# Conditional layer on quarters of TensorE, and contexts issued with every second group's scores

## The chip, the cores and the metric

The kernel runs on one core of a Trainium2 chip. Time is the device time of one execution in microseconds (us). The core has a matrix engine (TensorE, PE in the profile, with its weight loads as PEld), a vector engine (VectorE, DVE), an activation engine (ScalarE, ACT), GpSimd (POOL) and a queue engine (SyncE, SP) that issues most DMAs. Each works through its own instructions in order and waits on semaphores for the others. PE writes its results to banks of the memory PSUM, from which DVE and ACT copy them to the on-chip memory SBUF.

## The reference, cut to what matters

```python
def cond(x, condition, weights):               # x: (64, 64, 1024)
    W = weights[condition]                     # one (64, 64) matrix for each of 64 batches
    return einsum('bct,bcd->bdt', x, W)
def attn(x, qkvw, qkvb, ow, ob):               # 32 heads of 32, attention over the 64 rows of a batch
    q, k, v = split(x @ qkvw + qkvb)
    probs = softmax(einsum('bhqd,bhkd->bhqk', q, k) / sqrt(32))
    return einsum('bhqk,bhkd->bhqd', probs, v) @ ow + ob
x = x + attn(cond(x, itok_B_0_15, weights))
x = x + ffn(cond2(x, itok_B_0_7))              # routed LoRA layer, then a quantized gated FFN
```

Everything is float32 apart from the quantized products. The change lies in `cond` and in the attention; what follows the attention is left as it is.

## The kernel before, in words

The 4096 rows (64 batches of 64) are worked in eight blocks of 512 rows, that is four tiles of 128 rows; a tile holds two batches. The function `attention` does all that is spoken of here.

The conditional layer of a block (`conditional`, lines 337 to 376) multiplies each tile with the matrices of its two batches. These stand as two 64x64 blocks on the diagonal of a 128x128 tile `wbd`, zero elsewhere, so that one 128x128 matmul serves both batches (line 350). A product is half a tile's columns: four such matmuls into one PSUM bank, eight products for a block. The results are copied to the quarters B11, B12, B21 and B22 of the block's activations, those of even tiles by DVE (line 356), of odd ones by ACT (line 358). Four sums T1 to T4 of these quarters follow on DVE (lines 366 and 371).

The projections to queries, keys and values use a Strassen-Winograd scheme: seven products of quarter matrices instead of eight, in the order 1, 6, 7, 5, 2, 4, 3 (`job`, line 378). Product 1 needs B11 and the weights' A11, product 6 needs T2 and the weights' sum S2, product 7 T3 and S3, product 5 T1 and S1, product 2 B21 and A12. They share four PSUM banks a, b, c, d. A query or key job (`rows_job`, line 428) has seven products of 4 matmuls, a value job (`values_job`, line 455) seven of 8. In block 0 the sums S1 to S4 of the raw weights are made on the way, four on one another (`sums`, lines 270 to 273), on DVE or POOL, and stored for the later blocks.

The attention itself goes by groups, two for each of four steps c of a block: `scores` (16 matmuls of 64x64, four of them side by side on the four quarters of the array, line 491), then on DVE and ACT a softmax (lines 503 to 515), a transposition by DMA (line 526, with copies on ACT at lines 521 and 533), then `context` (16 matmuls of 128x64, two side by side, line 543). ACT copies a context out and sends it to DRAM (lines 553 and 554). The pool of its copies `co` has two buffers, that of the turned probabilities `pT` four, that of the contexts' PSUM banks two.

What stands where in each engine's instruction order is set by a planner written out in the file. `run` keeps a planned time `now` and adds each product's planned cost; before each product it issues whatever is due by that time (`at`). A product's copies out of PSUM, its `rest`, are issued only after the next product (`behind`). A group begins at its due time: first its scores, then every context whose probabilities are ready.

The four-bank pool `ps_g` is a ring that the conditional layer and all projections share: a product that wants a bank waits until what lay in it has been copied out. In the last step of a block the fills are the next block's conditional layer, its first value job and its first query and key jobs; in the last block of all they are the first products of the output projection, with the last contexts at a fixed planned time (`at(now + 41, contexts)`, line 699).

```python
                    ps = ps_g.tile([P, 4, P], F32, tag="g", name=f"cond_{b}_{j}_{hf}")
                    for q in range(KQ):
                        k = hf * KQ + q
                        nc.tensor.matmul(ps[:, q, :], xt[:, k * P:(k + 1) * P], wbd[j], start=True, stop=True)
```

## Time and profile before

| what | value |
|---|---|
| time of three runs | 2479.37, 2483.23, 2483.56 us (median 2483.23) |
| time of the profiled execution | 2482.55 us, its span 2480.8 us |
| PE busy | 2435.7 us (98%), 13232 matmul records |
| DVE busy | 1524.9 us (61%) |
| ACT busy | 953.6 us (38%) |
| conditional layer on PE (line 350) | 512 records of 128x128, 62.5 us |
| scores (line 491), contexts (line 543) | 2048 records each, 70.7 and 73.5 us |

A float32 matmul appears as two records. "Busy" counts a matmul to its modelled end. An idle time in the views is given with the instruction that ended it.

### The profile page before, as it was taken

Reading aid. Unit: us, or ns where it says so; the run is one execution under the profiler, and the core shown is the slowest. Engines: PE = TensorE matmul, PEld = TensorE weight load, DVE = VectorE, ACT = ScalarE, POOL = GpSimd, SP = SyncE. Lnnn points to the kernel's source line nnn. Section 1 sums busy time; section 2 is a strip of 40 time slices with the busy share of each in tenths; the row PEclk is TensorE's granted clock in tenths of the full one; section 3 lists DMA queues with packets and bytes.
Section 4 is the critical chain, followed back from the end, with each engine's and each line's share of the span. In section 5 each row is a group of like instructions: output and inputs, shape, how many; then the busy total and the mean of one; then the engine's idle time right before and its main releaser. Section 6 shows DMA issues by size and latency. Waiting matters only on the chain.

```text
span 2480.8 us, 34182 instructions
## 1 busy us (share of the span) xinstructions
PE 2435.7 (98%) x13232; PEld 1703.8 (69%) x13232; DVE 1524.9 (61%) x2957; ACT 953.6 (38%) x1303; POOL 360.8 (15%) x451
## 2 busy tenths in 40 slices
PE   8999999999999999999999999999999999999996
PEld 7888888888888888888888644444454545454452
DVE  4585585675764755745646623333367777778787
ACT  1243353443443533533534533343423333333333
POOL 5010011011122221110000233334200000000001
PEclk9999999999999999999999999999999999999997
DMA  8795767676677667766646668877744443434343
GB/s 281 262 266 153 225 192 232 191 208 203 205 201 246 206 188 248 201 202 181 171 145 215 187 213 248 271 232 239 227 151 79 87 79 81 85 73 91 71 96 70
DMA packets 417980, 446.76 MB, mean 180 GB/s; under 512 B 299665, under 2 KB 353938, under 8 KB 404114
## 3 DMA queue, kind: packets, MB, share of 16 engines
q1 hardware_dynamic: 387298, 377.90, 52.5%
q0 software_dynamic: 12080, 49.82, 7.6%
q10 hardware_dynamic: 18432, 16.79, 2.0%
q8 instruction: 106, 1.74, 0.3%
q14 instruction: 64, 0.52, 0.1%
HBM read 272.97 MB, written 100.66 MB: 151 GB/s over the span
## 4 chain that ended last, share of the span: by engine, by line
PE 95%; DVE 3%; DMA 1%; issue 1%; ACT 0%; SPq 0%; ACTq 0%; DVEq 0%
PE pska L428 5%; PE psva L455 5%; PE poc L1019 5%; PE pskc L428 4%; PE psvc L455 4%; PE pskd L428 4%; PE psqd L428 4%; PE pbc L1019 4%; PE pba L1019 4%; PE psvd L455 4%; PE psqa L428 4%; PE poa L1019 4%; PE pod L1019 4%; PE pbd L1019 4%; PE psqc L428 4%; PE s L491 3%
## 5 line engine op out<-in xcount | busy, mean ns | idle before, releaser
L533 ACT COPY pT<-phT 128x1024 int16<-128x1024 int16 x128 | 167.2, 1342 | 84.8 <-DMA phT<-ph 84.6
L553 ACT ACTIVATE co<-c,bqkv 128x256 f32<-128x256 f32 x128 | 60.6, 473 | 295.2 <-PE c L543 253.6
L503 DVE TENSOR_REDUCE mx<-s 128x8 f32<-128x512 f32 x128 | 88.3, 690 | 138.0 <-PE s L491 128.4
L521 ACT COPY ph<-prob 128x1024 int16<-128x1024 int16 x128 | 131.4, 1046 | 43.4 <-DVE prob L515 42.7
L414 DVE SCALAR_TENSOR_TENSOR kbd<-pskd,bqkv,psku 32x256 f32<-32x256 f32 x256 | 122.6, 479 | 30.9 <-PE pskd L428 27.2
L507 ACT ACTIVATE prob<-prob 128x512 f32<-128x512 f32 x128 | 78.9, 628 | 154.4 <-DVE prob L504 130.6
L1140 POOL TENSOR_TENSOR xo<-xo,ob 128x1024 f32<-128x1024 f32 x32 | 82.5, 2597 | 375.7 <-DMA xo<-in_x_dram 371.2
L428 PE MATMUL psqa<-yB,wq 128*128 128x256 f32 x512 | 123.5, 384 | 0.0
L428 PE MATMUL pska<-yB,wk 128*128 128x256 f32 x512 | 122.6, 382 | 0.0
L1483 POOL DMA_DIRECT2D out_dram<-y x29 | 25.2, 869 | 653.4 <-DVE y L1475 653.4
L1114 ACT COPY xh<-xo 128x1024 int16<-128x1024 int16 x64 | 64.1, 1040 | 143.8 <-DVE xo L1159 143.4
L455 PE MATMUL psva<-wv,yB 128*128 128x256 f32 x512 | 117.7, 383 | 0.0
L1019 PE MATMUL poa<-woA,cx 128*128 128x512 f32 x256 | 115.3, 593 | 0.0
L1019 PE MATMUL pba<-wtA,x1T 128*128 128x512 f32 x256 | 115.1, 592 | 0.0
L1125 ACT COPY xTo<-xhT 128x1024 int16<-128x1024 int16 x64 | 84.8, 1341 | 64.1 <-DMA xhT<-xh 62.3
L455 PEld LDWEIGHTS psva<-wv,yB 128*128 128x128 f32 x512 | 96.8, 191 | 13.4
L428 PEld LDWEIGHTS pska<-yB,wk 128*128 128x128 f32 x512 | 96.0, 190 | 14.3 <-issue 1.4
L428 PEld LDWEIGHTS psqa<-yB,wq 128*128 128x128 f32 x512 | 95.2, 190 | 13.7 <-issue 0.2
L513 DVE TENSOR_REDUCE den<-prob 128x8 f32<-128x512 f32 x128 | 86.8, 678 | 17.4 <-ACT prob L507 17.2
L504 DVE TENSOR_TENSOR prob<-s,mx 128x512 f32<-128x512 f32 x128 | 88.6, 692 | 9.7 <-DVE mx L503 0.9
L515 DVE TENSOR_TENSOR prob<-prob,den 128x512 f32<-128x512 f32 x128 | 89.8, 702 | 4.4
L412 ACT ACTIVATE kbd<-pska,bqkv 32x256 f32<-32x256 f32 x128 | 59.6, 466 | 79.2 <-PE pska L428 77.6
(243 smaller groups left out, 5138.5 us busy)
## 6 DMA issues: line engine op xcount, KB each, us to landing
wv<-v_d SPq DMA_DIRECT2D x98, 512.0 KB, 3.8
wq<-q_d SPq DMA_DIRECT2D x28, 1792.0 KB, 8.1
wk<-k_d SPq DMA_DIRECT2D x28, 1792.0 KB, 8.2
x<-in_x_dram SPq DMA_DIRECT2D x32, 512.0 KB, 9.8
ctx_d<-co ACTq DMA_DIRECT2D x128, 128.0 KB, 5.6
cx<-ctx_d SPq DMA_DIRECT2D x16, 1024.0 KB, 7.0
xo<-in_x_dram SPq DMA_DIRECT2D x32, 512.0 KB, 5.7
xT_d<-xTo SPq DMA_DIRECT2D x64, 256.0 KB, 4.1
```

The lines of the kernel that those rows point to most:

```text
L414: nc.vector.scalar_tensor_tensor(dst, ps, bias, u, ALU.add, ALU.add)
L428: nc.tensor.matmul(ps[:, 0:HB], A[:, SLOT[A_OF[i]], k, :], B[B_OF[i]][:, k, :], start=first and k == 0, stop=k == KQ - 1, skip_group_check ...
L455: nc.tensor.matmul(ps[:, j * VC:(j + 1) * VC], B[B_OF[i]][:, k, j * P:(j + 1) * P], A[:, k, :], start=first and j == 0 and k == 0, stop=k ...
L503: nc.vector.tensor_reduce(mx_v, ps, AX.X, ALU.max)
L504: nc.vector.tensor_tensor(p.rearrange("p (a e) k -> p a e k", a=2), ps, mx_v.unsqueeze(3).to_broadcast([P, 2, HPC, C]), ALU.subtract)
L513: nc.vector.tensor_reduce(den, p, AX.X, ALU.add)
L515: nc.vector.tensor_tensor(p, p, den.unsqueeze(2).to_broadcast([P, n, C]), ALU.mult)
L521: nc.scalar.copy(h, planes(p.rearrange("p n k -> p (n k)")))
L533: nc.scalar.copy(planes(pT.rearrange("p a b q -> p (a b q)")), hT)
L1019: self.nc.tensor.matmul(ps, self.B[self.B_OF[i]][:, k, :], self.A[self.A_OF[i]][:, k, :], start=first and k == 0, stop=k == self.KQ - 1, s ...
L1125: nc.scalar.copy(planes(xT.rearrange("p k q -> p (k q)")), hT)
L1140: nc.gpsimd.tensor_add(s["x"][:, t, :], s["x"][:, t, :], self.ob)
```

## The change

Each conditional product is now a whole tile: for each of eight column blocks, four 64x64 matmuls on the four quarters of the array, straight from the gathered matrices. It fills two banks, one for each batch of the tile, and is emptied by two DVE and two ACT copies of half the size. `wbd`, its clearing and its copies are gone. The sums T1 to T4 all stand after the last tile's copies. The planned cost of a tile is 1.2 where its two halves had 0.95 each; a block's first value job so has all seven products ahead of the second group of that step, where it had six.

A group issues the last product's copies right after its scores, and contexts only if two or more are ready. Their copies on ACT are spread in planned time. `pT` has six buffers, `co` a pool of its own with four. In block 0 the weight sums are issued one or two at a time between products, and the first query job takes its products in the order 1, 2, 6, 7, 5, 4, 3. The last contexts stand 3.5 later in planned time, one product of the output projection.

```diff
-        pTp = pool(ctx, "pT1", 4, side="right")
+        pTp = pool(ctx, "pT1", 6, side="right")
+        cop = pool(ctx, "co1", 4, side="right")
...
-        def sums(eng, at):
-            eng.tensor_tensor(at("S1"), at("A21"), at("A22"), ALU.add)
-            eng.tensor_tensor(at("S2"), at("S1"), at("A11"), ALU.subtract)
-            eng.tensor_tensor(at("S3"), at("A11"), at("A21"), ALU.subtract)
-            eng.tensor_tensor(at("S4"), at("A12"), at("S2"), ALU.subtract)
+        def sums(eng, at, stored):
+            def last():
+                eng.tensor_tensor(at("S4"), at("A12"), at("S2"), ALU.subtract)
+                stored()
+            return [
+                lambda: eng.tensor_tensor(at("S1"), at("A21"), at("A22"), ALU.add),
+                lambda: eng.tensor_tensor(at("S2"), at("S1"), at("A11"), ALU.subtract),
+                lambda: eng.tensor_tensor(at("S3"), at("A11"), at("A21"), ALU.subtract),
+                last,
+            ]
...
-        first_sums = [load_qk(0, "q", 0), load_qk(0, "k", 0, nc.gpsimd)]
+        first_sums = load_qk(0, "q", 0) + load_qk(0, "k", 0, nc.gpsimd)
-        first_sums.append(load_v_raw(0, nc.gpsimd))
-        wbd = []
-        for j in range(PB):
-            t = w.tile([P, P], F32, tag=f"wbd{j}", name=f"wbd{j}")
-            nc.vector.memset(t, 0.0)
-            wbd.append(t)
+        first_sums += load_v_raw(0, nc.gpsimd)
...
-            def one(hf, j):
-                key = f"B{hf + 1}{j // 2 + 1}"
-                box = []
+            def one(j):
+                banks = []
                 def product():
-                    xt = tiles[j][0]
-                    if j % 2 == 0:
-                        B[key] = yp.tile([P, KQ, HB], F32, tag=key, name=f"y{key}_{b}")
-                    ps = ps_g.tile([P, 4, P], F32, tag="g", name=f"cond_{b}_{j}_{hf}")
-                    for q in range(KQ):
-                        k = hf * KQ + q
-                        nc.tensor.matmul(ps[:, q, :], xt[:, k * P:(k + 1) * P], wbd[j], start=True, stop=True)
-                    box.append(ps)
+                    xt, wg = tiles[j]
+                    for r in range(2):
+                        banks.append(ps_g.tile([P, KC, C], F32, tag="g", name=f"cond{r}_{b}_{j}"))
+                    for k in range(KC):
+                        for r, f in ((0, 0), (1, 1), (0, 1), (1, 0)):
+                            nc.tensor.matmul(
+                                banks[r][halves[f], k, :], xt[halves[r], k * P + f * C:k * P + (f + 1) * C],
+                                wg[halves[r], :], start=True, stop=True,
+                            )
                 def rest():
-                    dst = B[key][:, :, (j % 2) * P:(j % 2 + 1) * P]
-                    if j % 2 == 0:
-                        nc.vector.tensor_copy(dst, box[0])
-                    else:
-                        nc.scalar.copy(dst, box[0])
-                    if (hf, j) == (0, 3):
+                    for hf in range(2):
+                        key = f"B{hf + 1}{j // 2 + 1}"
+                        if j % 2 == 0:
+                            B[key] = yp.tile([P, KQ, HB], F32, tag=key, name=f"y{key}_{b}")
+                        for r in range(2):
+                            t0 = (j % 2) * P + r * C
+                            src = banks[r][:, hf * KQ:(hf + 1) * KQ, :]
+                            if r == 0:
+                                nc.vector.tensor_copy(B[key][:, :, t0:t0 + C], src)
+                            else:
+                                nc.scalar.copy(B[key][:, :, t0:t0 + C], src)
+                    if j == PB - 1:
                         t_of("T1", "B12", "B11")
-                    elif (hf, j) == (1, 3):
                         t_of("T2", "B22", "T1")
                         t_of("T3", "B22", "B12")
-                    elif (hf, j) == (1, 1):
                         B["T4"] = B["B12"]
                         nc.vector.tensor_tensor(B["T4"], B["B21"], B["T2"], ALU.subtract)
-                return 0.95, product, rest
+                return 1.2, product, rest
             def t_of(key, x, y):
                 B[key] = yp.tile([P, KQ, HB], F32, tag=key, name=f"{key}_{b}")
                 nc.vector.tensor_tensor(B[key], B[x], B[y], ALU.subtract)
-            for j, (_, wg) in enumerate(tiles):
-                for r in range(2):
-                    (nc.gpsimd if b else nc.vector).tensor_copy(wbd[j][halves[r], halves[r]], wg[halves[r], :])
-            return [one(0, j) for j in range(PB)] + [one(1, j) for j in (2, 3, 0, 1)]
...
+        def job(name, cost, n, matmuls, put, begin=None, done=None, order=ORDER):
...
-                    if i == ORDER[0] and begin:
+                    if i == order[0] and begin:
                         begin()
+                    if order[1] == i == 2:
+                        behind.pop()()
...
-            return [one(i) for i in ORDER]
+            return [one(i) for i in order]
...
-        def context(b, c, us, pTs):
+        def context(b, c, us, pTs, wait):
...
-            for n, u in enumerate(us):
+            def copied(n, u):
                 m, t = UNITS[u]
                 ch = m * NP + c
-                co = p2.tile([P, HB], F32, tag="co", name=f"co_{b}_{c}_{u}")
+                co = cop.tile([P, HB], F32, tag="co", name=f"co_{b}_{c}_{u}")
                 nc.scalar.activation(co, pc[:, n, :], AF.Identity, bias=bqkv[:, 2 * KC + ch:2 * KC + ch + 1])
                 nc.scalar.dma_start(ctx_d[2 * b + t][:, ch, :], co)
+            for n, u in enumerate(us):
+                if wait:
+                    at(now + wait, lambda n=n, u=u: copied(n, u))
+                else:
+                    copied(n, u)
...
-        def contexts():
-            while waiting and len(waiting[0][3]) == 2:
-                context(*waiting.pop(0))
+        def contexts(least=1):
+            ready = sum(len(pTs) == 2 for *_, pTs in waiting)
+            for n in range(ready if ready >= least else 0):
+                context(*waiting.pop(0), 1.7 * n * (least - 1))
         def group(b, c, us):
             def begin():
                 ps = scores(b, c, us)
-                contexts()
+                if behind:
+                    behind.pop()()
+                contexts(2)
                 pTs = []
                 waiting.append((b, c, us, pTs))
...
-                        f = load_qk(*qk_jobs[n + 2])
-                        if f:
-                            pending_sums.append(f)
-                js = rows_job(b, c, wh, next_load)
+                        pending_sums.extend(load_qk(*qk_jobs[n + 2]) or [])
+                js = rows_job(b, c, wh, next_load, (1, 2, 6, 7, 5, 4, 3) if n == 0 else ORDER)
                 if b == 0 and n >= 2:
-                    cost, product, rest = js[5]
-                    def product_and_sums(product=product):
-                        product()
-                        if pending_sums:
-                            pending_sums.pop(0)()
-                    js[5] = (cost, product_and_sums, rest)
+                    for at_, count in ((5, 2), (6, 2)):
+                        with_sums(js, at_, pending_sums, count)
                 fills += js
             return fills
...
                 nxt = (b, g + 1) if g + 1 < NV else (b + 1, 0)
                 if nxt[0] < NBLK:
                     load_v(*nxt, slot)
             js = values_job(b, g, next_load)
             if (b, g) == (0, 0):
-                cost, product, rest = js[4]
-                def product_and_sums():
-                    product()
-                    pending_sums.pop(0)()
-                js[4] = (cost, product_and_sums, rest)
+                with_sums(js, 4, pending_sums, 4)
             return js
         for f in conditional(0, x_next):
...
                     if c == 0:
                         fills[7:7] = v_fill(b, 1)
                         if b == 0:
-                            cost, product, rest = fills[4]
-                            def with_sums(product=product):
-                                product()
-                                v_raw.pop()()
-                            fills[4] = (cost, with_sums, rest)
+                            for at_ in range(3, 7):
+                                with_sums(fills, at_, v_raw, 1)
                 elif b + 1 < NBLK:
                     fills += conditional(b + 1, x_next) + v_fill(b + 1, 0) + qk_fill(b + 1, 0)
...
                     op.open_rest()
                     fills += op.pair(0) + op.pair(1)
                     length = 24
-                    at(now + 41, contexts)
+                    at(now + 44.5, contexts)
                 if b + 1 == NBLK and c == 1:
                     assert next(chores, None) is None
                     early.close()
```

More of the change, by code (lines that the diff above doesn't have):

```diff
@@ L284, in load_qk @@
                     nc.sync.dma_start(t[:, SLOT[key], :, :], quarter(key, (0 if wh == "q" else H) + c * P, P))
-                def rest():
-                    sums(eng or nc.vector, lambda key: t[:, SLOT[key], :, :])
-                    nc.gpsimd.dma_start(qk_d[wh, c], t)
-                return rest
+                return sums(
+                    eng or nc.vector, lambda key: t[:, SLOT[key], :, :], lambda: nc.gpsimd.dma_start(qk_d[wh, c], t)
+                )
             nc.sync.dma_start(t, qk_d[wh, c])
@@ L303, in load_v_raw, with stored @@
                 nc.sync.dma_start(at(key), quarter(key, 2 * H + g * VC, VC))
-            def rest():
-                sums(eng, at)
+            def stored():
                 for slot in range(7):
                     later.append(lambda slot=slot: nc.gpsimd.dma_start(v_d[g][:, slot, :, :], w_v[0, g, slot]))
-            return rest
+            return sums(eng, at, stored)
         bqkv = act.tile([P, 3 * KC], F32, tag="bqkv", name="bqkv")
         x_next = load_x(0)
-        first_sums = [load_qk(0, "q", 0), load_qk(0, "k", 0, nc.gpsimd)]
+        first_sums = load_qk(0, "q", 0) + load_qk(0, "k", 0, nc.gpsimd)
         nc.sync.dma_start(bqkv, a["qkvb_t"])
-        first_sums.append(load_v_raw(0, nc.gpsimd))
-        wbd = []
-        for j in range(PB):
-            t = w.tile([P, P], F32, tag=f"wbd{j}", name=f"wbd{j}")
-            nc.vector.memset(t, 0.0)
-            wbd.append(t)
+        first_sums += load_v_raw(0, nc.gpsimd)
         kbd, vbd = [], []
@@ L337, in conditional @@
         def conditional(b, tiles):
-            def one(hf, j):
-                key = f"B{hf + 1}{j // 2 + 1}"
-                box = []
+            def one(j):
+                banks = []
                 def product():
-                    xt = tiles[j][0]
-                    if j % 2 == 0:
-                        B[key] = yp.tile([P, KQ, HB], F32, tag=key, name=f"y{key}_{b}")
-                    ps = ps_g.tile([P, 4, P], F32, tag="g", name=f"cond_{b}_{j}_{hf}")
-                    for q in range(KQ):
-                        k = hf * KQ + q
-                        nc.tensor.matmul(ps[:, q, :], xt[:, k * P:(k + 1) * P], wbd[j], start=True, stop=True)
-                    box.append(ps)
-                def rest():
-                    dst = B[key][:, :, (j % 2) * P:(j % 2 + 1) * P]
-                    if j % 2 == 0:
-                        nc.vector.tensor_copy(dst, box[0])
-                    else:
-                        nc.scalar.copy(dst, box[0])
-                    if (hf, j) == (0, 3):
+                    xt, wg = tiles[j]
[6 more added lines that the diff above has]
+                                wg[halves[r], :], start=True, stop=True,
+                            )
+                def rest():
+                    for hf in range(2):
[10 more added lines that the diff above has]
+                    if j == PB - 1:
@@ L371, in t_of @@
                 nc.vector.tensor_tensor(B[key], B[x], B[y], ALU.subtract)
-            for j, (_, wg) in enumerate(tiles):
-                for r in range(2):
-                    (nc.gpsimd if b else nc.vector).tensor_copy(wbd[j][halves[r], halves[r]], wg[halves[r], :])
-            return [one(0, j) for j in range(PB)] + [one(1, j) for j in (2, 3, 0, 1)]
-        def job(name, cost, n, matmuls, put, begin=None, done=None):
+            return [one(j) for j in range(PB)]
+        def job(name, cost, n, matmuls, put, begin=None, done=None, order=ORDER):
             banks, u = {}, {}
@@ L414, in biased, with rows_job @@
                 nc.vector.scalar_tensor_tensor(dst, ps, bias, u, ALU.add, ALU.add)
-        def rows_job(b, c, wh, next_load):
+        def rows_job(b, c, wh, next_load, order=ORDER):
             qT = None
@@ L445, in done @@
                     next_load()
-            return job(f"ps{wh}{{}}_{b}_{c}", 1.72, HB, matmuls, put, begin, done)
+            return job(f"ps{wh}{{}}_{b}_{c}", 1.72, HB, matmuls, put, begin, done, order)
         def values_job(b, g, next_load):
@@ L627, in next_load, with with_sums, product_and_sums @@
                     if n + 2 < len(qk_jobs):
-                        f = load_qk(*qk_jobs[n + 2])
-                        if f:
-                            pending_sums.append(f)
-                js = rows_job(b, c, wh, next_load)
+                        pending_sums.extend(load_qk(*qk_jobs[n + 2]) or [])
+                js = rows_job(b, c, wh, next_load, (1, 2, 6, 7, 5, 4, 3) if n == 0 else ORDER)
                 if b == 0 and n >= 2:
-                    cost, product, rest = js[5]
-                    def product_and_sums(product=product):
-                        product()
-                        if pending_sums:
-                            pending_sums.pop(0)()
-                    js[5] = (cost, product_and_sums, rest)
+                    for at_, count in ((5, 2), (6, 2)):
+                        with_sums(js, at_, pending_sums, count)
                 fills += js
             return fills
+        def with_sums(fills, i, sums, count):
+            cost, product, rest = fills[i]
+            def product_and_sums():
+                for _ in range(min(count, len(sums))):
+                    sums.pop(0)()
+                product()
+            fills[i] = (cost, product_and_sums, rest)
         v_raw = []
@@ L650, in next_load @@
                     if slot == SLOT[A_OF[ORDER[-1]]]:
-                        v_raw.append(load_v_raw(g + 1, nc.vector))
+                        v_raw.extend(load_v_raw(g + 1, nc.vector))
                     return
```

## The prediction

> **What bounds the kernel now.** I first read busy times, and the chain that ended last.

> ```profile
> PE 2435.7 (98%) x13232; PEld 1703.8 (69%) x13232; DVE 1524.9 (61%) x2957; ACT 953.6 (38%) x1303; POOL 360.8 (15%) x451
> ...
> PE 95%; DVE 3%; DMA 1%; issue 1%; ACT 0%; SPq 0%; ACTq 0%; DVEq 0%
> ```

> TensorE sets the time, so only its own work and its waits count. Its waits:

> ```profile
> PE cond L350 <- DVE wbd L375: 9.2, 1, 9.2
> ...
> PE c L543 <- ACT pT L533: 5.9, 1, 5.9
> ...
> PE cond L350 <- DVE yB L356: 3.2, 7, 0.5
> PE psqd L428 <- DVE qT L414: 3.0, 1, 3.0
> ```

> (Total us, times, longest.) Apart from 1.6 us in the first query job and the kernel's very end these are nearly all, and the seven of 0.5 us lie in the very stage that the change speeds up. Here is that stage in block 4, as the chain of work shows it (start, us, what):

> ```profile
> 696.69 1.08 PE s L491 x32
> ...
> 697.79 0.70 DVE mx L503
> ...
> 698.59 0.69 DVE prob L504
> 699.28 0.38 DVE kbd L414
> ...
> 701.18 0.69 DVE yB L356
> ...
> 702.58 0.69 DVE prob L504
> 703.27 0.61 DVE yB L356
> ...
> 703.92 2.94 PE cond L350 x24
> ```

> For 6 us the chain is on DVE, not on PE. In the 17 us from 696.6 DVE is busy for most of it (columns: length, then PE, PEld, DVE, ACT, POOL busy):

> ```profile
> 696.60:713.60 17.00, 16.55 (x161) 15.30 (x161) 14.97 (x23) 9.01 (x13) 1.83 (x4) 1.00 0.53 175
> ```

> **The change part by part.** The sum is made against the profiled execution, 2482.55 us, which lies 0.7 below the median of the runs.

> *Quarter matmuls, PE alone.* PE's rows in the timeline of this stage (start, length):

> ```profile
> 696.62 1.10 PE L491 MATMUL s<-kbd,qT 64*64 64x128 f32 x32
> 697.66 1.15 PE L543 MATMUL c<-pT,vbd 128*64 128x64 f32 x32
> 698.74 4.73 PE L350 MATMUL cond<-wbd,x 128*128 128x128 f32 x40
> ...
> 706.70 3.65 PE L455 MATMUL psva<-wv,yB 128*128 128x256 f32 x16
> ...
> 710.19 3.62 PE L455 MATMUL psvb<-wv,T 128*128 128x256 f32 x16
> ```

> and, in a window only 21 ns wide (615.345 to 615.366), four score matmuls that start in it:

> ```profile
> 615.35 0.34 PE L491 MATMUL s<-kbd,qT 64*64 64x128 f32 x4
> ```

> Four quarters start together. Contexts, 64 columns like the new matmuls, take 32 records as 16 pairs in 1.15 - 0.22 (the last one's length) = 0.93 us, 58 ns a pair. A new tile is 8 column blocks x 2 records = 16 such slots: 0.93 us, 3.8 us a block with a switch of tiling at 0.1. Now a block takes 706.70 - 698.74 = 7.96. PE alone would save 4.1 us a block, 33 in all. [...]

> *What DVE and ACT make of it.* I lay the stage out from the scores' start (block 4: 696.62 = 0), in the order in which the changed program issues. PE: scores 1.03, two contexts (now one) to 3.05, tile 0 to 4.0, tile 1 to 5.0. Each tile has two banks of four, so tile 2 needs tile 0's copies done, tile 3 tile 1's. DVE: the key job's last four copies come first now, 4 x 0.48, to 2.3; max and subtract 0.69 + 0.69 with gaps, to 3.8; two copies of tile 0 to 5.1 (0.42 each, the 128x256 row of line 402, since the new copies have 256 elements; a half of line 356's 0.69 would be 0.34, taken as the low end); max, subtract to 6.6; tile 1 to 7.5; sum, reciprocal, multiply (0.68, 0.20, 0.69) to 9.2; tile 2 to 10.1, tile 3 to 11.0; T1 and T2 (1.22 each) to 13.5. ACT: context copy plus DMA issue 0.87 each, two to 3.8 (from 2.1), exponent to 4.5, tile 0 (0.36 each, line 399) to 5.3, two more context copies to 7.0, exponent 7.7, tile 1 to 8.5. So tile 2 starts at 5.3, tile 3 at 8.5 instead of 6.2; the value job wants tile 2's first bank (10.1) and starts at 10.15, its product 6 at 13.64, when product 1 (3.49) is done and T2 just so. Before, product 6 starts at 710.19 - 696.62 = 13.57 with one context in front. Without contexts (2.02 after, 1.08 before) that is 11.62 against 12.49: 0.9 us saved of 4.1. Six blocks have this form: 5.2. In block 1 no context stands there and the layout gives product 6 at 13.26 against 12.49: 0.8 lost. Sum -4.4. With DVE and ACT copies of 0.36 and 0.30 product 6 comes at 13.2, with 0.46 and 0.42 at 14.0: ends -7.5 and -2. If DVE's cover ended there, T2 would be late next, and each us of it is PE's.

> The late tail on DVE (T3, T4, then the second unit's sum and multiply at 17.7 instead of 12.1) puts its transposition behind by 5.6 us; its context starts some 20 us later, so that is hidden. The removed `wbd` copies stood on POOL, idle there: nothing. SP gets one value load earlier in its order, which waits for a product that PE has by then done: nothing.

> *Start.* PE waits to 9.19 for `wbd`; the gather itself lands at 8.67. Tiles 0 and 1 then run at the half clock (granted until 12.1), tile 3 ends near 14.3 (17.82 now). Product 1 ends at 16.1, product 2 waits for ACT's copy of bank a and ends at 18.4; DVE has the four sums (2.75) and the copies ahead of T1 and T2, so T2 is ready at 20.4 and product 6 starts at 20.5, against 21.34, with product 2 done already (1.73). -2.6; a later T2 costs its delay, so between 0 and -4.

> *Block 0.* The 3.0 us wait for `qT` comes from four value sums of 1.22 in front of it on DVE. Two are left in front; DVE reaches `qT` at 80.2 where PE wants its bank at 79.65: 0.6 remains. The clock behind it:

> ```profile
> 80.40:83.80 3.40, 0.95 (x4) 1.00 0.58 131
> 83.80:87.20 3.40, 3.40 (x9) 0.50 0.04 6
> 18.90:22.40 3.50, 1.88 (x9) 1.00 1.09 348
> ```

> (Length, PE busy, granted clock.) After 3.4 us with PE busy for 0.95 the next 3.4 ran at half clock, 1.7 lost. So 3.2 + 1.7 - 0.6: -4.3.

> *Rest before softmax.* A 0.6 us wait of `psqd` for value copies behind a softmax goes: -0.6.

> *Paired contexts.* A context alone takes 1.08 us to the next start, two together 2.02: 0.15 for each entry saved. 56 entries become 31: -3.7. One triple (block 1) finds its third PSUM bank held until ACT's first two copies end: +0.7.

> *Last contexts.* PE waits 5.9 us for `pT`, then runs at half clock; one projection product (3.43, in the trace 5.2 with the slow clock) moves ahead of it. ACT's copies of the first of now three contexts must end before the third, near 1438-1439, and PE still idles some 3.5 us, so the slow clock may come again: -3, between 0 and -7.

> *Clock in the new stage.* PE idles 2.2 us before tile 3 and 0.7 after, so some 3.4 us windows have it busy for 1.0 to 1.3. [...] The trace halved it at 0.95 busy and not at 1.88. I take three of seven stages, at 1.7: +5; ends 0 and +12.

> Sum: -4.4 - 2.6 - 4.3 - 0.6 - 3.7 + 0.7 - 3 + 5 = -12.9, so 2469.7, and with the median's 0.7 about 2470 us.

> **The rivals.**

> *PE's saving comes through.* If DVE kept up, seven blocks would give 4.1 instead of 0.6 and no slow clock: about 2440, half of it 2453. For: PE is the bound overall. Against: DVE's 14.97 of 17 us.

> *Nothing measurable.* Clock halved once in each of seven stages (+12 instead of +5) and the copies at their long end (+3): about 2480.

> *Slower.* The slow clock holds for two windows, as after the 5.9 us wait for `pT` (granted clock 0.50 from 1435.5 to 1442.3), in all eight conditional stages: 8 x 3.4 = 27 instead of 5, about 2492. It decides from 2.2 us a stage, where it outweighs the 18 saved. For: PE works through short pieces between waits. Against: the value products behind the stage are full work, and one full window at 83.8 restored the clock.

> *The quarters don't run side by side.* Then the layer would take 4 x 58 ns a slot, 15 us a block, and about 2530. The four starts exclude it as good as.

> **How the numbers follow.** DVE-bound stage with some slow windows 0.55 (2470, own range 2459 to 2478); saving comes through, wholly or half, 0.12; nothing measurable 0.15; slower 0.18. What a measurement here can tell from no change is 0.2%, 5 us, so these give faster 0.67, same 0.15, slower 0.18. The range 2450 to 2491 leaves out the far part of the first and last rival.

> **What would show it.** Line 349's records near 3.8 us of PE work a block, spread over 7 us from scores to value job; PE waits on `yB` copies by DVE and ACT of some 2 us a block, up from 0.5; the wait for `qT` below 1; 31 context entries. Granted clock below 1 in stretches of 3.4 us near the conditional stages tells the clock's part. I am wrong if PE runs through the four tiles without waits, or if value products wait for T2 by more than 1 us.

## The result: 0.44% slower

The changed kernel takes 2493.43 us (median of 5 runs, 2492.77 to 2495.5); the kernel before took 2480.36 us beside it (5 runs, 2478.49 to 2483.56). The ratio is 1.0044, 95% interval 1.0032 to 1.0056. The prediction was 2470 with a range of 2450 to 2491: the sign is wrong and the time lies outside the range.

From the page of the changed kernel, its span, its busy times and the row of its instruction queue:

```profile
span 2491.9 us, 37331 instructions
...
PE 2423.2 (97%) x14768; PEld 1690.7 (68%) x14768; DVE 1540.8 (62%) x2977; ACT 956.3 (38%) x1335; POOL 348.4 (14%) x395
...
q8 instruction: 118, 1.93, 0.3%
```

TensorE is busy for 12.5 us less than before (2435.7), and still the span is 11.1 us longer: TensorE's idle time, the span less the busy time, rose from 45.1 to 68.7 us. What it waits for (total us, times, longest):

```profile
PE cond L349 <- issue: 24.1, 11, 5.0
...
PE c L547 <- ACT co L558: 6.5, 2, 6.0
...
PE cond L349 <- ACT yB L365: 2.7, 2, 1.6
PE psqb L432 <- DVE T L376: 1.9, 1, 1.9
```

The waits for `qT` (3.0) and for `vbd` that the change was to remove are gone. New is the first row: 24.1 us in the quarter matmuls, and it names no engine and no data. "issue" is time in which the engine waited for nothing that the profile shows.

This is the conditional stage of block 4 on TensorE (start, length, number of records):

```profile
700.06 1.10 PE L495 MATMUL s<-kbd,qT 64*64 64x128 f32 x32
701.10 2.08 PE L547 MATMUL c<-pT,vbd 128*64 128x64 f32 x64
703.11 2.73 PE L349 MATMUL cond<-wg,x 64*64 64x64 f32 x151
710.80 3.05 PE L349 MATMUL cond<-wg,x 64*64 64x64 f32 x105 [4.96 <-issue]
713.78 4.62 PE L459 MATMUL psva<-wv,yB 128*128 128x256 f32 x16
718.24 3.62 PE L459 MATMUL psvb<-wv,T 128*128 128x256 f32 x16
```

A tile is 64 records. TensorE stops after 151, in the middle of the third tile, where no operand changes hands, stands still for 4.96 us and then goes on. The same stage in windows of the clock (length, TensorE busy, granted clock, DMA share, GB/s):

```profile
705.42:708.83 3.41, 0.42 (x23) 1.00 0.90 311
708.83:712.24 3.41, 1.44 (x53) 0.50 0.26 79
712.24:715.65 3.41, 3.41 (x67) 0.50 0.00 0
```

After a window with 0.42 us of work the clock was halved for two windows, and the value product behind (`psva`) took 4.62 us instead of 3.65. In attention up to the last block's scores the clock was halved once at the start (at 22.7 us) and in each of the seven later conditional stages, for 37.5 us in all; before, in none of these places, and only once elsewhere (at 83.8 us).

What comes in while TensorE stands still is in the DMA rows of two windows of this stage. In 700.0 to 708.2 no row of the instruction queue q8 stands:

```profile
q1 hardware_dynamic: 996, 2.05, 85.3%
q0 software_dynamic: 52, 0.19, 5.7%
q10 hardware_dynamic: 146, 0.14, 4.8%
...
wk<-k_d SPq DMA_DIRECT2D x1, 1792.0 KB, 8.7
```

and in the half microsecond from 708.2 there is one:

```profile
q8 instruction: 1, 0.02, 12.0%
```

This packet starts at 708.28, takes 0.96 us, and 1.6 us after its end TensorE goes on. Before it, the engines had been moving the next block's key weights (1.8 MB, issued at the start of the stage, landed 8.7 us later) at about 300 GB/s.

How large a packet is follows from two pages. The page of the kernel before has

```profile
q8 instruction: 106, 1.74, 0.3%
```

and now there are 118 packets, with 2 x (14768 - 13232) = 3072 more TensorE instructions, matmuls and weight loads. That is 256 for each of the 12 more packets, and 1.93 MB / 118 = 16 KB each. A new tile's 64 matmuls with their 64 weight loads take 64 x 18 ns = 1.16 us (151 records in 2.73 us), so the layer uses up a packet in 2.3 us.

That each of these waits is one for a packet can be counted. In the trace of the changed kernel, nine of the eleven "issue" waits of the layer, 23.7 of the 24.1 us, end when 449, 3009, 5825, 8897, 11713, 14529, 14785, 17601 and 20417 instructions of TensorE (PE and PEld with their semaphore instructions) have begun. Each of these numbers is 193 more than a multiple of 256, though the places within the layer differ (after 106 to 231 of its 256 records), and each wait ends 0.8 to 1.6 us after an instruction packet has landed.

### The profile page after: what moved, and what is told of

Its sections match the earlier page's. It is cut to its first block, busy times and chain, and to the rows that moved or that the text cites. A ratio compares the mean times of both kernels' runs of the same rounds, so it can differ in the third digit from the quotient of the medians.

```text
span 2491.9 us, 37331 instructions
## 1 busy us (share of the span) xinstructions
PE 2423.2 (97%) x14768; PEld 1690.7 (68%) x14768; DVE 1540.8 (62%) x2977; ACT 956.3 (38%) x1335; POOL 348.4 (14%) x395
## 3 DMA queue, kind: packets, MB, share of 16 engines
q8 instruction: 118, 1.93, 0.3%
## 4 chain that ended last, share of the span: by engine, by line
PE 94%; DVE 2%; issue 1%; DMA 1%; ACT 1%; SPq 0%; ACTq 0%; DVEq 0%
PE psva L459 5%; PE psvd L459 4%; PE psvc L459 4%; PE pska L432 4%; PE pbc L1026 4%; PE pba L1026 4%; PE psqa L432 4%; PE psqc L432 4%; PE psqd L432 4%; PE pskc L432 4%; PE pbd L1026 4%; PE pskd L432 4%; PE pod L1026 4%; PE poa L1026 4%; PE poc L1026 4%; PE c L547 2%
## 5 line engine op out<-in xcount | busy, mean ns | idle before, releaser
L459 PE MATMUL psva<-wv,yB 128*128 128x256 f32 x512 | 123.5, 396 | 0.0
L508 DVE TENSOR_TENSOR prob<-s,mx 128x512 f32<-128x512 f32 x128 | 88.5, 691 | 10.2 <-ACT prob L511 0.5
L474 DVE TENSOR_TENSOR vbd<-psvd,psvu 64x256 f32<-64x256 f32 x128 | 54.0, 422 | 63.3 <-PE psvd L459 61.9
```

The lines of the kernel that those rows point to most:

```text
L459: nc.tensor.matmul(ps[:, j * VC:(j + 1) * VC], B[B_OF[i]][:, k, j * P:(j + 1) * P], A[:, k, :], start=first and j == 0 and k == 0, stop=k ...
L508: nc.vector.tensor_tensor(p.rearrange("p (a e) k -> p a e k", a=2), ps, mx_v.unsqueeze(3).to_broadcast([P, 2, HPC, C]), ALU.subtract)
```

## The experiments

Theory S: TensorE runs out of instructions, because a packet of 256 is used up (here in 2.3 us) faster than the next arrives behind other DMA traffic; the clock is then halved after the idle time. Rival E, the prediction's own: the copies of the tiles out of PSUM on DVE and ACT bound the stage, and the clock falls from those waits.

### The layer on quarters undone

```
-        for r, f in ((0, 0), (1, 1), (0, 1), (1, 0)):
-            nc.tensor.matmul(banks[r][halves[f], k, :], xt[halves[r], ...], wg[halves[r], :], ...)
+        for q in range(KQ):
+            nc.tensor.matmul(ps[:, q, :], xt[:, k * P:(k + 1) * P], wbd[j], start=True, stop=True)
```

with the layer's padded weights, copies and costs of before; all else as changed.

> Everything of the change but the quarter conditional layer: that layer is again 64 matmuls of 128x128 a block on zero-padded weights. Theory S (supply of instructions: 256 conditional matmuls and their 256 weight loads a block come to TensorE in packets of 256 instructions, each some 4.3 us late behind other DMA traffic, so TensorE starves and its clock halves): the loss goes, about 2471 us, 22 below the changed kernel and 9 below the kernel before; 'issue' waits of the conditional line near 0, clock below 1 only at the start and near the end. Theory E (the stage is bound by copies out of PSUM on DVE and ACT, and the clock falls from these waits): the same about 2471. If the block-0 order, the contexts or the end carry the loss instead: 2493 or near it.

Measured: 2467.28 us (4 runs), ratio to before 0.9954 (0.9938 to 0.9971). The rest of the change saves 11.4 us, and the layer on quarters alone turns this into a loss. No "issue" wait of the layer is left, and the clock falls in no conditional stage. S and E are not told apart by this.

### The layer on quarters alone

The diff above the other way round, in the kernel before.

> The kernel before with only the conditional layer on quarters, nothing else of the change. Both S and E: about 2500 us, 20 above the kernel before, with clock falls in all eight conditional stages and over 15 us of 'issue' waits in that line. If the layer on quarters harms only together with two contexts in the stage: within 5 us of 2480.

Measured: 2502.43 us (4 runs), ratio 1.0099 (1.0077 to 1.0121); "issue" waits in the layer 19.7 us, and half clock in six of the seven later stages. The layer costs the same without two contexts in its stage: 24 us here, 26 inside the change (2493.43 against 2467.28, by their ratios 1.0044 and 0.9954 some 22). So the pair of contexts in front of it in the changed kernel is not the reason.

### Half as many instructions

```
-                        for r, f in ((0, 0), (1, 1), (0, 1), (1, 0)):
+                        for r in range(2):
                             nc.tensor.matmul(
-                                banks[r][halves[f], k, :], xt[halves[r], k * P + f * C:k * P + (f + 1) * C],
+                                banks[r][:, k, :], xt[halves[r], k * P:(k + 1) * P],
                                 wg[halves[r], :], start=True, stop=True,
```

> The changed kernel with each column block of the conditional layer as two matmuls 64x128 (the two row halves side by side in two banks) instead of four 64x64: 64+64 instructions more than before a block become 128+128 in all instead of 256+256, same banks, same copies, same order. S: 'issue' waits of that line fall from 24 us to under 6, fewer clock falls, 2472 to 2480 us. E: same copies, same waits, 2490 to 2493.

Measured: 2484.38 us (11 runs), ratio 1.0022 (1.0013 to 1.0031). The "issue" waits of the layer are gone altogether, and with the same copies the kernel is faster than the changed one, by 9 us or, by the ratios, some 5, so E's "no change" falls. But 2484 lies above the 2472 to 2480 expected of S. In its trace the layer in block 4, and at the start:

```profile
704.56 5.79 PE L349 MATMUL cond<-wg,x 64*128 64x64 f32 x98
710.67 2.00 PE L349 MATMUL cond<-wg,x 64*128 64x64 f32 x30 [0.33 <-ACT yB L365]
...
10.10 13.92 PE L349 MATMUL cond<-wg,x 64*128 64x64 f32 x128 [10.10 <-DMA wg<-in_condw_dram,idx]
```

A pair of these matmuls takes 118 ns (98 records in 5.79 us), so the layer needs 8.04 us to the value product, no less than the 7.96 of the padded one. And at the start it ran wholly at half clock, which was raised only at 27.45 us, against 12.5 in the changed kernel; the first scores began at 74.9 us instead of 69.0. The missing waits are S's. Of the 4 to 12 us above its forecast, 6 lie in this start in the profiled execution; neither theory had it, and why the clock stayed low there is open.

### The key load moved away

The next block's key weights are loaded some 14 us later in planned time; the layer, its instructions and its copies stay as changed.

```
...
+                    if qk_jobs[n] == (b, "k", NP - 1):
+                        at(now + 14, lambda: load_qk(*qk_jobs[n + 2]))
+                    else:
                         pending_sums.extend(load_qk(*qk_jobs[n + 2]) or [])
```

> The changed kernel with the 1.8 MB load of the next block's key weights issued some 14 us later, so that it no longer runs beside the conditional stage. S: the packets of instructions come sooner (lag 4.3 toward 2 us), 'issue' waits fall from 24 us to some 8, clock falls in fewer stages, 2478 to 2486 us. E: no change, 2492 to 2494.

Measured: 2466.2 us (4 runs), ratio 0.995 (0.9933 to 0.9966): the loss is not halved, as expected, but gone. TensorE's waits and block 4's stage in its trace:

```profile
PE cond L349 <- ACT yB L365: 5.5, 6, 1.6
...
PE cond L349 <- issue: 3.8, 6, 1.4
```

```profile
689.68 1.10 PE L495 MATMUL s<-kbd,qT 64*64 64x128 f32 x32
690.72 2.08 PE L547 MATMUL c<-pT,vbd 128*64 128x64 f32 x64
692.73 2.73 PE L349 MATMUL cond<-wg,x 64*64 64x64 f32 x151
696.31 0.91 PE L349 MATMUL cond<-wg,x 64*64 64x64 f32 x43 [0.85 <-issue]
697.71 1.16 PE L349 MATMUL cond<-wg,x 64*64 64x64 f32 x62 [0.49 <-ACT yB L365]
698.79 3.72 PE L459 MATMUL psva<-wv,yB 128*128 128x256 f32 x16
```

and of its instruction queue from 693.7 to 694.2 us:

```profile
q8 instruction: 1, 0.02, 15.8%
```

TensorE stops after the same 151 records, but for 0.85 us instead of 4.96, and the clock stays full. The packet now starts 4.1 us after the scores (693.75), not 8.2, and in each of the seven later stages the packet comes 2.6 to 4.1 us sooner after the scores than in the changed kernel. (The lag of 4.3 us that the expectation names is an estimate, the median in the changed kernel's trace from TensorE's 128th instruction past a multiple of 256 to the start of the next packet; here it comes out at 3.3, not near 2.) The "issue" waits fall from 24.1 to 3.8 us, and beyond the start the clock falls in two conditional stages instead of seven. The span is 26.9 us shorter: by the pages 15.6 less idle time of TensorE (53.1 against 68.7) and 11.3 less busy time (2411.9 against 2423.2). This trace lacks 38 matmul records of the quantized FFN (14730 against 14768), so about 2 us of busy time count as idle; up to the FFN it is 17.6 less idle and 9.3 less busy time, and the latter is the half clock's part.

### The same load moved in the kernel before

The load may have hurt in another way than by TensorE's instructions. The same edit, in the kernel before:

> The kernel before, with only the 1.8 MB key load issued some 14 us later in each block. Theory S (the load hurts by holding up TensorE's instruction packets, which only the layer on quarters needs fast): no gain, 2476 to 2482 us. Rival L (moving this load is worth 12 us or more by itself, whatever the layer): 2464 to 2470.

Measured: 2481.57 us (14 runs), ratio 1.0014 (1.0006 to 1.0023). Nothing is gained there; it is rather 0.14% slower. The load costs only where the layer on quarters needs its instructions fast, and L falls. With the three runs before this settles it for S: without the small matmuls, or with half of them, the "issue" waits go; without the traffic in front of their packets they fall to 3.8 us.

### Start: GpSimd held off

In the changed kernel GpSimd's sums of the key weights begin at 19.4 us instead of 23.9, beside VectorE's T sums. From its trace:

```profile
18.73 1.21 DVE L376 TENSOR_TENSOR T<-yB,yB 128x1024 f32<-128x1024 f32 x1
19.39 1.67 POOL L276 TENSOR_TENSOR wk<-wk 128x512 f32<-128x512 f32 x1
20.04 2.10 DVE L376 TENSOR_TENSOR T<-yB,T 128x1024 f32<-128x1024 f32 x1
21.14 2.13 POOL L277 TENSOR_TENSOR wk<-wk 128x512 f32<-128x512 f32 x1
22.07 2.28 DVE L376 TENSOR_TENSOR T<-yB,yB 128x1024 f32<-128x1024 f32 x1
```

T2, which product 6 wants, takes 2.10 us where the first T sum took 1.21. The edit, on top of the later key load, lets the key sums start only when T3 is written:

```
-        for f in first_sums:
+        for f in first_sums[:4]:
             f()
+        rest_sums = [lambda: held(w_qk[0, "k", 0][:, SLOT["S1"], 0, 0:1], B["T3"][:, 0, :])] + first_sums[4:]
...
+        with_sums(fills, 3, rest_sums, len(rest_sums))
```

> The changed kernel with the later key load (2466), and at the start the key-weight sums of GpSimd held until VectorE's T3 is written, so that they no longer run beside VectorE's T sums. If GpSimd's work is what stretches a T sum from 1.22 to 2.1 us and makes product 6 wait: T sums at 1.2, the 2.1 us wait of psqb falls to about 1, no clock fall at 23 us, 2462 to 2464. If the stretch is something else: 2466.

```profile
18.86 6.96 POOL L687 MEMSET vbd<- 128x4096 f32 x2
19.54 1.23 DVE L376 TENSOR_TENSOR T<-yB,T 128x1024 f32<-128x1024 f32 x1
20.68 1.22 DVE L376 TENSOR_TENSOR T<-yB,yB 128x1024 f32<-128x1024 f32 x1
...
20.82 1.99 PE L432 MATMUL psqb<-T,wq 128*128 128x256 f32 x8
```

The T sums are back at 1.22 us, product 6 starts at 20.82 instead of 22.20, its wait for T is gone, and the clock no longer falls at 23 us; the first scores come 3.0 us sooner than with the later key load alone. The mechanism is shown. In the total, 2465.0 us (4 runs, ratio 0.9945, 0.9928 to 0.9962) cannot be told from 2466.2, and the forecast of 2462 to 2464 is missed: the profiled span is only 2.5 us shorter.

### End: the last transposition ahead on its queue

In the changed kernel the last context waits 5.95 us for ACT's copies of the first one, and these stand on ACT behind a copy that waits for the last transposition:

```profile
1429.96 1.03 ACT L525 COPY ph<-prob 128x1024 int16<-128x1024 int16 x1
...
1442.51 1.74 SPq L530 DMA_TRANSPOSE phT<-ph  x1
...
1449.45 1.34 ACT L537 COPY pT<-phT 128x1024 int16<-128x1024 int16 x1 [8.37 <-DMA phT<-ph]
1450.66 0.47 ACT L558 ACTIVATE co<-c,bqkv 128x256 f32<-128x256 f32 x1
...
1452.06 1.97 PE L547 MATMUL c<-pT,vbd 128*64 128x64 f32 x32 [5.95 <-ACT co L558]
```

Its input `ph` is ready at 1431.0, but SyncE issues it at 1442.5, behind the first pair's stores and loads. The edit, on top of the later key load:

```
                 h = parted(b, c, u, p)
+                if (b, c, u) == (NBLK - 1, NP - 1, 3):
+                    third(u, turned(b, c, u, h), pTs)
+                    return
...
-                    at(now + 44.5, contexts)
+                    at(now + 32, contexts)
+                    at(now + 41, contexts)
```

> The changed kernel with the later key load (2466), and at the end of attention the last unit's transposition issued on SyncE's queue ahead of the first pair's stores and loads (now it is issued 11.5 us after its input is ready), and two of the last three contexts ahead of the last one. If that queue is what makes the last context late: the 5.7 us wait before it goes and with it the 6.8 us of half clock, 2455 to 2459. If the wait only moves to another transfer: 2463 to 2467.

Measured: 2461.11 us (4 runs), ratio 0.9931 (0.9915 to 0.9948), 5 us less than with the later key load alone and between the two forecasts; the intervals of the two kernels overlap. The transposition is issued in time and the wait falls, but to 2.1 + 0.5 us, not to nothing: the `pT` copies now stand on ACT behind four copies of contexts (line 558). The half clock is 3.4 us long instead of 6.8. The edit moves two things, the transposition on its queue and two contexts, whose copies so stand earlier on ACT; which of them brings the gain is not shown. ACT's order is late next. In the profiled executions only 2.8 us of the gain lie behind the last scores, another 2.3 come from before them, where this execution kept its full clock at the start.

### Both, and what the quarters are worth then

> Both edits together on the changed kernel with the later key load: the sum of the two, 2452 to 2456 us if both hold.

Measured: 2459.95 us (4 runs), ratio 0.9929 (0.9912 to 0.9945). It beats both kernels; the parts do not add up to the 2452 to 2456 expected. Then once more, beside the change without quarters but with the edited end:

> The kernel with everything of the change but the layer on quarters (2467), and the same edit of the end of attention as in the run of the later key load with that end (-5 there). 2462 to 2464. It asks whether the layer on quarters is worth anything at all once its instructions come in time.

> The changed kernel with later key load, start and end edits once more, on the same chip as the kernel without quarters but with the same end: 2458 to 2462. Six stages at about 0.8 us less and the edited start make it 2 to 4 us faster than that kernel; if the layer on quarters is worth nothing, the two are within 1 us.

Measured on one chip: 2463.57 us without quarters (5 runs, ratio 0.9937, 0.9923 to 0.9951) and 2459.94 with them (5 runs, ratio 0.9928, 0.9914 to 0.9941). The 3.6 us are of the size expected, but the intervals overlap, and the second kernel also has the later key load and the edited start: that the layer on quarters is worth anything is likely, not shown. In the two profiled executions the start is 1.8 us shorter with quarters, the seven later stages 5.4 us, and the time from the last but one scores on is 3.5 us longer, for a reason that is open.

## Why the prediction was wrong, step by step

- *The conditional stage and its clock* is the step that failed. "Quarter matmuls", "What DVE and ACT make of it" and "Clock in the new stage" came to -4.4 + 5 = +0.6 us for the seven later stages. By the marks of the score groups in the traces, these stages cost 22.4 us more than in the kernel with the layer undone. The sum had terms for TensorE's slots, PSUM banks, DVE, ACT and the clock, and none for the supply of TensorE's instructions, which cost 23.7 us of waits and most of the half clock behind them. The number was at hand: the page before had 106 instruction packets, about 250 instructions each if TensorE's 2 x 13232 are divided by them; with 512 instructions of the layer to be issued in 3.8 us, as the prediction had it, the next packet has 1.9 us to arrive. The waits that the prediction named as the sign that it holds, for `yB` copies some 2 us a block, came out at 2.7 us in all.
- *What the stage is worth when its instructions arrive* was right in the net. With the key load moved, the five stages whose clock stayed full are on average 0.9 us shorter than with the layer undone (0.4, 1.2, 0.6, 1.1, 1.4); the prediction had 0.9. But two errors cancel in it, which is luck: TensorE's work in the layer takes 1 us a block more than forecast (next point), and the waits for copies are 5.5 us in all, not some 2 us a block.
- *The slot of the quarters* was mis-sized: 151 records in 2.73 us are 72 ns for four, not 58, and the layer takes 4.8 us, not 3.8. That four quarters would keep the distance of a pair of contexts was the author's estimate.
- *Clock.* Here the half clock came in the seven later stages and once at the start, as the rival "slower" had it in eight. Up to the FFN TensorE's busy time was 9.3 us above that with the later key load (which itself has 10.2 us of half clock there), between the 5 of the sum and the rival's 27. That rival's 2492 is near the result, but for another reason: it looked for the idle time in short pieces between waits for copies, and had no idle stretch of 5 us.
- *Start*: -2.6 forecast, +0.8 measured in the changed kernel. The wait for `wbd` went as told, but TensorE waited for instructions once (0.87 us), and the T sums, moved to run beside GpSimd's sums, took 2.1 us. The prediction had placed T2 by durations measured while GpSimd did nothing. With GpSimd held, product 6 starts at 20.8; the forecast was 20.5.
- *Block 0*: -4.3 forecast, -5.0 measured (from the first scores to the second), in the changed kernel and in the one with the layer undone alike. Right.
- *Paired contexts*: the marks move by -1.08 and +0.93 in turn, a net 0.15 for each entry saved, as forecast.
- *End*: -3 forecast, -0.2 measured from the last scores to the end of the span (1080.25 and 1080.04 us). The wait moved from `pT` to the context copies behind the same `pT` on ACT. The prediction had seen that these copies must end first, and had not looked at what stands ahead of them on ACT, nor at SyncE's queue ahead of the transposition.
- Without the layer on quarters the other terms sum to -10.9 (block 0, rest, contexts, triple, end), and that kernel measures -11.4. Their sum was right, with block 0 worth more than forecast and the end less (1.7 us); what was missed is the layer on quarters.

## What to carry to other kernels

Here TensorE waited 23.7 us for instructions, not for data. Where many small matmuls replace few large ones, divide the instruction packets of the page into the engine's instruction count (256 each here), and compare the time in which a packet is used up (2.3 us in this layer) with the time in which one arrives beside the large transfers of that stage (in block 4, 8.2 us after the scores beside the key load and 4.1 without it). Here an "issue" wait in the middle of a row of matmuls with the same operands was the sign of it, and moving a large load out of the way (3.8 us of these waits left), or having half as many instructions (none left), the cure. When an edit moves work on one engine earlier, ask also which engine it now runs beside, and take the duration of that pairing (here 2.10 us instead of 1.22 for a T sum).
